# Scan order, opening by chunks, and the place of beside work in the attention rounds of a two-layer hybrid kernel

## The chip, the cores and the metric

The kernel runs on one core of a Trainium2 chip. The metric is the device time of one execution in microseconds. Before the change it is 11721.87 us, the median of three runs (11714.78 to 11722.49).

## What is computed

Input is `x`, four images of 64 x 64 pixels with 128 channels, all in fp32. Cut to what matters (weights left out of the argument lists):

```
# layer 0, on the group-normalised image: three selective scans over 4096 tokens
xz  = in_proj(x)                                  # 2 x 256 channels
y   = mamba(xz) + flip(mamba_b(flip(xz))) + unslice(mamba_s(slice(xz)))
x   = x + out_proj(y * silu(z))
#   mamba: conv of 4 taps, silu, delta = softplus(...), and the scan
#   h = h * exp(delta * A) + delta * u * B ;  y = sum_n h * C + D * u     (16 states)

# layer 1, on tokens t (4 images x 4096 tokens; the attention is over all 4096 of an image)
q   = ring(cos(layernorm(t) + theta))             # 16 heads of 8; q is query, key and value
a   = softmax(q q^T / sqrt(8)) q                  # per head, 4096 x 4096
x1  = layernorm(u + a w_comb + b)                 # u = layernorm(t)
t   = t + layernorm(x1 + w2 relu(w1 cos(x1[:8]) + b1) + b2)
# experts: each of 64 experts takes the 8 likeliest tokens of an image,
#   pools them, runs an MLP of 128-512-128, and adds the answer back to those tokens
```

## The kernel before

The work is a Python program that records instructions in an order of its own: generators yield small steps, and a `Pace` runs so many steps of each generator beside the attention rounds. What stands earlier in the program stands earlier in each engine's queue. The stages, with their place in the profiled execution:

1. **Head**, 0 to 2176 us. `Inputs` makes u, delta, B and C for all images (`pieces`, line 264; `of_chunk`, line 357) beside the scans of image 0 (`Scans.of_image`, line 457). Then `opening(0)` makes the tokens of image 0.
2. **Loops 0 to 2**, one per image (`Attention.loop`, line 875): attention of image b, beside it the scans of image b + 1, then `after(b - 1)` (line 985: output projection, feed-forward, the experts' logits), then `opening(b + 1)` (line 815).
3. **Loop 3**: attention of image 3 by query block; beside it `after(2)`, the experts' search and pooling for images 0 to 2, and `after(3)` for blocks that are done.
4. **Tail**, 250 us: the last block's `after`, the experts' answers, the scatter.

**A loop** has 1024 rounds, one for each group of 4 heads, block of 512 queries and block of 128 keys. In a round, `scores` (line 914) issues 4 score matmuls (line 924) into two PSUM tiles `s` and two exponentials `e` (line 929) of 128 x 1024 on ScalarE (ACT). `values` (line 932) issues 4 value matmuls (line 938, each executed as two) that add into one PSUM bank `acc`. Every 32 rounds `sums` copies `acc` to `av` (line 947), and three rounds later `store` writes it out by GpSimd's (POOL) queue (lines 953, 956). Lines 968 to 980 set the order of a round i: scores of round i + 1, values of round i, `av` at a block's end, stores, then `beside(i)`, which runs steps of the other generators. PSUM has three `s` tiles, one `acc` and one bank for all beside work (`Bank`, line 126): a step takes the bank with `yield PE`, so the caller knows that the step which follows is a piece of TensorE (PE) work, and `leave`s it after the copy out of it.

**The scans** go by order (0 forward, 1 backward, 2 slices), chunk of 1024 tokens (`T`; 4 chunks, `NC`), 8 blocks of 32 channels and 4 steps: 384 steps an image. A step loads delta and du two steps ahead on SyncE's (SP) queue (line 489), takes an exponential on ACT (line 503, `dA` or `delta`), and on VectorE (DVE) multiplies by B (line 510), scans (line 519) and multiplies by C (line 524). In two of four steps `total` (line 551) sums over states on PE into `y`: 16 matmuls, executed in one go with the step's exponential. `out` (line 556) adds D * u and stores a block of 32 channels by POOL's queue into one DRAM tile for each image and order. `product` (line 528) makes du for the next chunk beside the steps; its loads (line 540) follow on SP behind its last store. `early` (line 210) names the chunks whose du `Inputs` makes itself.

**The opening** of an image has 8 groups of 512 tokens. `tokens` (line 742) loads the three scans' sums and the gate `sz` (lines 750, 758, on SP), adds and multiplies them on DVE (line 763), projects by `out` on PE (line 771), normalises and starts the angles. `heads` and `rings` (lines 831, 841) make q: a transposition `qT` on PE (line 863), a split in two on DVE (lines 866, 867) and six stores on SP (line 871). In `beside` of `tile_kernel` (line 1478) the opening is run only once all scan steps of its image are done (`left == 0.0`); what is left after round 1023 is run between the loops (lines 1495 to 1499).

**`after`**, block by block: `co` (line 1041), `zt` (1062), `h` (1076, matmuls with 8 rows), `fo` (1087), `xT` (1109), `lg` (1119). The experts' pooling has `wt` (1254) and `pool` (1265). Each is one piece on PE between two yields. In loop 3 all this goes at 0.92 steps a round (line 1519), and what is left then runs behind the loop (`last.rest()`).

Of the kernel before, what the change touches and what calls it, by code (L numbers as in the profile page):

```python
# [23 lines left out]
SLICES = 16  # L24
T = 1024
# [183 lines left out]

def early(b, order, c):  # L210

    return b == 0 or (b == 1 and order == 0 and c < 2)
# [15 lines left out]
class Inputs:  # L228
# [35 lines left out]
    def pieces(self, images):  # L264

        for b in images:
            self.sz[b] = self.dram.tile([DI, L], F32, name=f"d_sz_{b}")
            yield self.norm(b)
            for order in range(3):
                if order == 2:  # L270
                    yield self.slices(b)
                for c in range(NC):
                    yield self.of_chunk(b, order, c)
                    third, at = divmod(order * NC + c, 3)
                    if at == 2:
                        yield self.gate(b, third)
# [156 lines left out]
class Scans:  # L433
# [6 lines left out]
    def __init__(self, tc, ctx, ws, ident, bank, dram):  # L440
        nc = self.nc = tc.nc
        self.ws, self.bank, self.dram = ws, bank, dram
        const = ctx.enter_context(tc.tile_pool(name="s_const", side="right", bufs=1))
        self.rows = ctx.enter_context(tc.tile_pool(name="s_rows", side="right", bufs=2))
        self.deep = ctx.enter_context(tc.tile_pool(name="s_deep", side="right", bufs=3))
        self.small = ctx.enter_context(tc.tile_pool(name="s_small", side="right", bufs=2))

        self.sel = const.tile([P, 2, 32], F32, name="sel")
        nc.vector.memset(self.sel, 0.0)
        for i in range(2):  # L450
            nc.vector.tensor_reduce(
                self.sel[:, i, 16 * i : 16 * i + 16], ident.rearrange("p (d n) -> p d n", n=NS2),
                mybir.AxisListType.X, ALU.add,
            )
        self.sums, self.steps, self.did = {}, {}, set()

    def of_image(self, b, made, alone=False):

        nc = self.nc
        self.steps[b] = 0  # L460
        for order in range(3):
            self.sums[b, order] = self.dram.tile([DI, L], F32, name=f"d_y_{b}_{order}")
        steps = [(order, c, k, j) for order in range(3) for c in range(NC) for k in range(8) for j in range(4)]
# [64 lines left out]
        def product(s):  # L528

            order, c, k, j = steps[s]  # L530
            part, turn = divmod(4 * k + j - 8, 3)
            chunk = (b, order, c + 1) if c + 1 < NC else (b, order + 1, 0) if order < 2 else (b + 1, 0, 0)
            if part < 0 or turn == 1 or chunk not in made or early(*chunk):
                return
            of, m, at = made[chunk], part // 4, part % 4 * (T // 4)
            cut = slice(m * P, (m + 1) * P), slice(at, at + T // 4)
            if turn == 0:
                for name in ("delta", "u"):
                    t = self.extra.tile([P, T // 4], F32, tag=f"x_{name}", name=f"x_{name}_{b}_{s}")
                    nc.sync.dma_start(out=t, in_=of[name][cut])  # L540
                    tiles["x", name] = t
            else:
                t, u = tiles.pop(("x", "delta")), tiles.pop(("x", "u"))
                nc.vector.tensor_mul(t, t, u)  # L544
                nc.gpsimd.dma_start(out=of["du"][cut], in_=t)  # L545
# [10 lines left out]
        def out(s, y):  # L556
# [10 lines left out]
            nc.vector.scalar_tensor_tensor(into, u, self.ws[order]["D"][:, k : k + 1], y, ALU.mult, ALU.add)  # L567
            to = self.sums[b, order][32 * k : 32 * k + 32]
            if order == 0:
                nc.gpsimd.dma_start(out=to[:, c * T : (c + 1) * T].rearrange("p (g t) -> g p t", g=4), in_=o)  # L570
                return
# [79 lines left out]
class Attention:  # L651
# [3 lines left out]
    def __init__(self, tc, ctx, w, gate, cols, ident, bank, dram, t1, w_out, sums, sz, x):  # L655
# [3 lines left out]
        self.w_out, self.sums, self.sz, self.x = w_out, sums, sz, x  # L659
# [51 lines left out]
        self.lag = 0  # L711
# [30 lines left out]
    def tokens(self, b, g, angles):  # L742
# [5 lines left out]
        cut, tiles = slice(g * 512, (g + 1) * 512), slice(g * 4, g * 4 + 4)  # L748
        x_g = self.piece([P, 4, C], "x_g", name=f"xr_{b}_{g}")
        nc.sync.dma_start(out=x_g, in_=xin[:, tiles, :])  # L750
        ys = []
        for m in range(2):
            rows = slice(m * P, (m + 1) * P)
            parts = []
            for i, src in enumerate([self.sums[b, order] for order in range(3)] + [self.sz[b]]):
                tag, bufs = ("y0", 2 * self.n) if i == 0 else (f"p{i - 1}", self.ahead)
                t = self.one.tile([P, 512], F32, tag=tag, bufs=bufs, name=f"y{i}_{b}_{g}_{m}")
                nc.sync.dma_start(out=t, in_=src[rows, cut])
                parts.append(t)
            yield  # L760
            y = parts[0]
            for t, op in zip(parts[1:], (ALU.add, ALU.add, ALU.mult)):
                nc.vector.tensor_tensor(y, y, t, op)
            ys.append(y)
# [26 lines left out]
        yield  # L791

# [82 lines left out]
    def loop(self, b, beside, by_block=False):  # L875


        nc = self.nc
        self.context[b] = self.dram.tile([P, L], F32, name=f"d_ctx_{b}")
# [64 lines left out]
        def sums(j, qb, i):  # L944

            av = self.mid.tile([P, QB], F32, tag="av", name=f"av_{b}_{j}_{qb}")
            nc.scalar.copy(av, accs.pop((j, qb)))  # L947
# [20 lines left out]
        for i, (j, qb, kc) in enumerate(rounds):  # L968
# [4 lines left out]
            values(i)  # L973
            if kc == NT - 1:
                sums(j, qb, i)
# [4 lines left out]
            beside(i)  # L980
        for i in sorted(later):
            later[i]()
        self.whole[b] = L // QB

    def after(self, b, gs=range(L // QB), to=None):
# [68 lines left out]
        def second(g):  # L1054
# [6 lines left out]
            for k in range(4):  # L1061
                nc.tensor.transpose(ps[:D, k * P : (k + 1) * P], z[:, g * 4 + k, :], self.ident)
# [11 lines left out]
            for f in range(4):  # L1074
                ps = yield from self.bank.take(f"h_{b}_{g}_{f}")
                nc.tensor.matmul(ps, self.w1[:, f * P : (f + 1) * P], zT, start=True, stop=True)  # L1076
# [7 lines left out]
            for k in range(4):  # L1084
                ps = yield from self.bank.take(f"fo_{b}_{g}_{k}")
                for f in range(4):
                    nc.tensor.matmul(  # L1087
                        ps[:, :C], h[:, f, k * P : (k + 1) * P], self.w2[:, f, :], start=(f == 0), stop=(f == 3)
                    )
# [18 lines left out]
            for k in range(4):  # L1108
                nc.tensor.transpose(ps[:, k * P : (k + 1) * P], u[:, k, :], self.ident)
# [9 lines left out]
            nc.tensor.matmul(ps[rows], self.gate, xT, start=True, stop=True)  # L1119
# [286 lines left out]
class Pace:  # L1406
# [4 lines left out]

    def run(self, share):
        self.credit += share
        while self.credit >= 1 and not self.done:
            self.credit -= 1
            self.then = next(self.parts, self)
            self.done = self.then is self
# [6 lines left out]
def tile_kernel(tc, ctx, x, in_proj_w, dirs, out_proj_w, attn, gate, weight1, weight2, out):  # L1424
# [32 lines left out]
    block = Attention(tc, ctx, attn, gate, cols, ident, bank, dram, t1, w_out, scans.sums, inputs.sz, x)  # L1457
# [14 lines left out]
    with tc.manual_schedule():  # L1472
        last = Pace()
        n = 3 * NC * NB
        for b in range(nb - 1):
            opens = Pace(block.opening(b + 1))

            def beside(i):
# [4 lines left out]
                following.run(min(1.3, max(0.5, left / max(1, 860 - i))))  # L1483
                other = last if not last.done else opens if left == 0.0 else None
                if other is None:
# [23 lines left out]
    with tc.manual_schedule():  # L1509
# [9 lines left out]
        block.loop(nb - 1, lambda i: last.run(0.92), True)  # L1519
        last.rest()  # L1520
    loop.close()
# [49 lines left out]
```

## Time and profile before

The profiled execution took 11713.44 us; its span is 11711.7 us. The other runs are the median and range above.

| stage | from - to (us) | PE busy | DVE busy | ACT busy | granted clock |
|---|---|---|---|---|---|
| head | 0 - 2175.6 | 1421.3 | 2016.3 | 1150.2 | 0.80 |
| loop 0 | 2175.6 - 4570.2 | 2224.1 | 2058.1 | 2326.4 | 0.98 |
| between | 4570.2 - 4614.7 | 8.2 | 37.1 | 7.3 | 0.63 |
| loop 1 | 4614.7 - 6976.9 | 2237.4 | 2065.1 | 2297.6 | 0.98 |
| between | 6976.9 - 7021.3 | 8.2 | 37.1 | 7.3 | 0.62 |
| loop 2 | 7021.3 - 9345.4 | 2217.1 | 1890.2 | 2258.2 | 0.98 |
| loop 3 | 9348.0 - 11461.8 | 2073.0 | 360.7 | 1939.3 | 0.99 |
| tail | 11461.8 - 11711.7 | 127.6 | 86.1 | 32.3 | 0.67 |

Over the whole span PE is busy 88%, ACT 86%, DVE 73%. A busy time is the union of an engine's instructions; both matmuls and exponentials overlap their successors, so a duration is longer than the time from one start to the next, and a share near 100% does not say that an engine never waits. The idle columns of the groups and the starts in the timeline say that. "<-" names what ended a wait. PEld is the loading of weights ahead of a matmul.

### The profile page before, as it was taken

What the parts mean: (1) busy time and instruction counts of PE and PEld (TensorE: products, weight loads), DVE (VectorE), ACT (ScalarE), POOL (GpSimd) and SP (SyncE); (2) the same over time, 40 slices, a digit from 0 to 9 for tenths busy, and PEclk for the clock granted to TensorE, in tenths of its full rate; (3) what the DMA queues carried; (4) which work ended last, traced back from release to release, by engine and by line L of the source; (5) the groups of instructions that cost most, each with busy time, mean ns of one, the idle gap of its engine ahead of it and who ended that gap; (6) DMA issues with size and microseconds to landing.
All of it is one profiled execution on the core that took longest, in us unless ns stands there. A gap on an engine that the chain in (4) does not pass through costs nothing.

```text
span 11711.7 us, 181745 instructions
## 1 busy us (share of the span) xinstructions
PE 10319.3 (88%) x68038; PEld 3430.9 (29%) x68038; DVE 8550.7 (73%) x8743; ACT 10019.7 (86%) x10604; POOL 3373.1 (29%) x4017
## 2 busy tenths in 40 slices
PE   6677674699999997999999979999999999999995
PEld 2222231222222232333333222333332223333323
DVE  7999998898988877998898879989887321101113
ACT  4565563699999997999999989999999999999992
POOL 5525362231323222324244223243341111000011
PEclk8888786799999998999999989999999999999997
DMA  6777777655565556665656566565555322222125
GB/s 186 219 222 209 212 209 204 174 152 154 150 155 147 145 161 173 158 157 147 156 140 154 150 176 168 152 153 142 150 138 137 120 93 67 75 70 76 59 73 187
DMA packets 835819, 1747.47 MB, mean 149 GB/s; under 512 B 141070, under 2 KB 373574, under 8 KB 834678
## 3 DMA queue, kind: packets, MB, share of 16 engines
q1 hardware_dynamic: 649438, 1318.65, 42.3%
q0 software_dynamic: 144000, 307.48, 8.5%
q10 hardware_dynamic: 41496, 109.71, 3.5%
q8 instruction: 534, 8.75, 0.3%
q14 instruction: 351, 2.88, 0.1%
HBM read 1379.76 MB, written 355.47 MB: 148 GB/s over the span
## 4 chain that ended last, share of the span: by engine, by line
PE 58%; DVE 13%; ACT 10%; issue 9%; DMA 8%; SPq 1%; POOL 0%; ACTq 0%; DVEq 0%; POOLq 0%
PE acc L938 33%; PE s L924 15%; ACT e L929 7%; DVE h L519 7%; PE y L551 4%; DMA delta<-d_delta 3%; DVE dB L510 2%; DMA du<-d_du 1%; PE fo L1087 1%; DVE du L510 1%; PE h L1076 1%; DMA y<-d_y 1%; PE cv L387 1%; DMA w<-in_L_ffn_weight_dram 1%; ACT dA L503 1%
## 5 line engine op out<-in xcount | busy, mean ns | idle before, releaser
L929 ACT ACTIVATE e<-s 128x1024 f32<-128x1024 f32 x8192 | 7777.3, 1102 | 357.9 <-PE s L924 313.0
L938 PE MATMUL acc<-e,val 128*32 128x512 f32 x32768 | 5676.3, 612 | 79.5 <-ACT av L947 78.7
L924 PE MATMUL s<-qm,key 32*128 32x512 f32 x16384 | 2784.7, 501 | 370.5 <-ACT e L929 310.5
L521 POOL COPY ends<-h 128x1 f32<-128x1 f32 x1152 | 1608.5, 1396 | 2597.6 <-DVE h L519 2590.9
L924 PEld LDWEIGHTS s<-qm,key 32*128 32x128 f32 x16384 | 1067.4, 183 | 3619.9 <-issue 1948.1
L938 PEld LDWEIGHTS acc<-e,val 128*32 128x32 f32 x32768 | 1028.4, 108 | 2009.7 <-issue 1015.4
L519 DVE TENSOR_TENSOR_SCAN h<-delta,ends,du 128x1024 f32<-128x1024 f32 x576 | 1353.5, 2350 | 86.3 <-ACT delta L503 77.1
L519 DVE TENSOR_TENSOR_SCAN h<-dA,ends,dB 128x1024 f32<-128x1024 f32 x576 | 1353.3, 2350 | 21.4 <-ACT dA L503 17.8
L503 ACT ACTIVATE dA<-delta,A 128x1024 f32<-128x1024 f32 x768 | 938.6, 1222 | 482.0 <-DMA delta<-d_delta 426.4
L510 DVE TENSOR_TENSOR dB<-du,B 128x1024 f32<-128x1024 f32 x768 | 931.8, 1213 | 549.8 <-PE y L551 370.1
L503 ACT ACTIVATE delta<-delta,A 128x1024 f32<-128x1024 f32 x768 | 938.9, 1222 | 75.3 <-PE y L551 68.4
L510 DVE TENSOR_TENSOR du<-du,B 128x1024 f32<-128x1024 f32 x768 | 925.6, 1205 | 28.7 <-DMA B<-d_bc 28.7
L524 DVE TENSOR_TENSOR dB<-h,C 128x1024 f32<-128x1024 f32 x768 | 939.6, 1223 | 0.0
L524 DVE TENSOR_TENSOR du<-h,C 128x1024 f32<-128x1024 f32 x768 | 939.4, 1223 | 0.1
L551 PE MATMUL y<-du,sel 128*32 128x256 f32 x6144 | 738.5, 404 | 184.1 <-DVE du L524 183.9
L551 PE MATMUL y<-dB,sel 128*32 128x256 f32 x6144 | 733.5, 400 | 91.6 <-DVE dB L524 40.9
L953 POOL DMA_DIRECT2D d_ctx<-av x512 | 260.7, 521 | 922.5 <-ACT av L947 912.7
L387 PE MATMUL cv<-xn,conv 128*128 128x512 f32 x1024 | 488.4, 632 | 20.0 <-DVE xn L322 20.0
L580 POOL DMA_DIRECT2D d_y<-o x512 | 329.6, 673 | 550.8 <-DVE o L567 489.9
L545 POOL DMA_DIRECT2D d_du<-x_delta x272 | 155.2, 571 | 1105.4 <-DVE x_delta L544 1029.2
L519 DVE TENSOR_TENSOR_SCAN h<-delta,du 128x1024 f32<-128x1024 f32 x192 | 439.2, 2287 | 13.1 <-ACT delta L503 7.1
L519 DVE TENSOR_TENSOR_SCAN h<-dA,dB 128x1024 f32<-128x1024 f32 x192 | 439.2, 2287 | 11.9 <-ACT dA L503 10.6
(245 smaller groups left out, 6450.8 us busy)
## 6 DMA issues: line engine op xcount, KB each, us to landing
delta<-d_delta SPq DMA_DIRECT2D x768, 512.0 KB
du<-d_du SPq DMA_DIRECT2D x576, 512.0 KB
du<-d_du ACTq DMA_DIRECT2D x192, 512.0 KB
key<-d_q SPq DMA_DIRECT2D x352, 256.0 KB
d_u<-u POOLq DMA_DIRECT2D x48, 1024.0 KB, 7.1
d_delta<-r POOLq DMA_DIRECT2D x48, 1024.0 KB, 6.5
B<-d_bc SPq DMA_DIRECT2D x96, 512.0 KB
C<-d_bc SPq DMA_DIRECT2D x96, 512.0 KB
```

The costliest lines, as they stand in the source:

```text
L387: nc.tensor.matmul(ps[:, cut], w["conv"][:, k, m * P : (m + 1) * P], reads(k, g), start=(k == 0), stop=(k == 3))
L503: nc.scalar.activation(tiles["delta", s], t, AF.Exp, scale=A)
L510: nc.vector.tensor_mul(tiles["du", s], du, spread[order, c, "B", j % 2])
L519: nc.vector.tensor_tensor_scan(h, dA, dB, first, ALU.mult, ALU.add)
L521: nc.gpsimd.tensor_copy(ends[order, c][:, at : at + 1], h[:, T - 1 :])
L524: nc.vector.tensor_mul(dB, h, spread[order, c, "C", j % 2])
L551: nc.tensor.matmul(y[32 * g : 32 * g + 32, : T // 4], self.sel[:, j // 2, :], hC[:, 256 * g : 256 * g + 256], start=(j == 0), stop=(j == 3),)
L580: nc.gpsimd.dma_start(out=to.rearrange("p (i j) -> p i j", i=SLICES)[:, :, at : at + n], in_=rows.rearrange("p (i j) -> p i j", i=SLICES),)
L924: nc.tensor.matmul(s_ps[:, k, :], keys[f"{i // 4}"][rows, cut].bitcast(F32R), queries[j, qb][rows, :].bitcast(F32R), start=True, stop=True,)
L929: nc.scalar.activation(e, s_ps, AF.Exp, scale=1.0 / math.sqrt(D))
L938: nc.tensor.matmul(accs[j, qb][32 * k : 32 * k + 32, :], v[:, k * VW : k * VW + 32], es[i][k // 2][:, k % 2, :], start=(kc == 0), stop=(kc ...
L953: nc.gpsimd.dma_start(out=self.context[b][h * D : h * D + D, cut], in_=av[32 * k : 32 * k + D, :])
```

## The change

Four things are changed together.

- **Order of scans.** Images 1 to 3 scan backward, slices, forward (`ORDERS`); `Inputs` makes their chunks in that order. The forward order's sums go to one DRAM tile a chunk instead of one for the image.
- **Opening by chunks.** `tokens` no longer waits for the whole scan: it goes on when the blocks stored (`stored`) reach chunk c of the forward order, two blocks later for all but the last chunk. It waits some rounds more between loads and sums (`settle(2)`). `beside` runs the opening as soon as `after` is done, in the same slots as `after`, and the scans are spread to round 890 instead of 860.
- **Place of beside work.** In all four loops `beside(i)` stands between the scores of round i + 1 and the values of round i. The store of `av` is moved with it.
- **Loop 3.** PE pieces of `after` are cut in two by `pause` (a `yield PE` while `cut` is set): `zt`, `h`, `fo`, `xT`, `lg`; `h` and `lg` become two matmuls of 256 columns. `turn` runs up to three steps a round with at most one PE piece, and no PE piece in every third round until 831. `av` is copied by DVE.

```diff
+ORDERS = {0: (0, 1, 2), 1: (1, 2, 0)}
...
+def orders(b):
+    return ORDERS[min(b, 1)]
...
-    return b == 0 or (b == 1 and order == 0 and c < 2)
+    return b == 0 or (b == 1 and order == orders(b)[0] and c < 2)
...
-        for order in range(3):
+        for order in range(1, 3):
             self.sums[b, order] = self.dram.tile([DI, L], F32, name=f"d_y_{b}_{order}")
+        for c in range(NC):
+            self.sums[b, 0, c] = self.dram.tile([DI, T], F32, name=f"d_y_{b}_0_{c}")
...
+            self.stored[b] += 1
+            if order == 0:
+                to = self.sums[b, order, c][32 * k : 32 * k + 32]
+                nc.gpsimd.dma_start(out=to.rearrange("p (g t) -> g p t", g=4), in_=o)
+                return
...
+        c, part = divmod(g, T // 512)
+        while self.scans.stored[b] < min(8 * (2 * NC + c + 1) + 2, 8 * 3 * NC):
+            yield WAIT
...
             yield
+            yield from self.settle(2)
             y = parts[0]
...
+    def pause(self):
+        if self.cut:
+            yield PE
...
-            nc.scalar.copy(av, accs.pop((j, qb)))
+            (nc.vector.tensor_copy if by_block else nc.scalar.copy)(av, accs.pop((j, qb)))
...
                 scores(i + 1)
-            values(i)
-            if kc == NT - 1:
-                sums(j, qb, i)
...
             if i in later:
                 later.pop(i)()
             beside(i)
+            values(i)
+            if kc == NT - 1:
+                sums(j, qb, i)
...
             for k in range(4):
+                if k == 2:
+                    yield from self.pause()
                 nc.tensor.transpose(ps[:D, k * P : (k + 1) * P], z[:, g * 4 + k, :], self.ident)
...
-                nc.tensor.matmul(ps, self.w1[:, f * P : (f + 1) * P], zT, start=True, stop=True)
+                for part in range(2):
+                    cols = slice(part * QB // 2, (part + 1) * QB // 2)
+                    if part:
+                        yield from self.pause()
+                    nc.tensor.matmul(ps[:, cols], self.w1[:, f * P : (f + 1) * P], zT[:, cols], start=True, stop=True)
...
                 for f in range(4):
+                    if f == 2:
+                        yield from self.pause()
                     nc.tensor.matmul(
                         ps[:, :C], h[:, f, k * P : (k + 1) * P], self.w2[:, f, :], start=(f == 0), stop=(f == 3)
...
+    def turn(self, share, free):
+        self.credit = min(self.credit + share, 3.0)
+        while self.credit >= 1 and not self.done and (free or self.then is not PE):
+            free = free and self.then is not PE
+            self.step()
...
-                following.run(min(1.3, max(0.5, left / max(1, 860 - i))))
-                other = last if not last.done else opens if left == 0.0 else None
-                if other is None:
+                following.run(min(1.3, max(0.5, left / max(1, 890 - i))))
+                other = opens if last.done else last
+                if other.done:
                     return
...
-        block.loop(nb - 1, lambda i: last.run(0.92), True)
+        block.loop(nb - 1, lambda i: last.turn(1.5, i % 3 > 0 or i > 830), True)
         last.rest()
+        block.cut = False
```

## The prediction

> **What bounds the kernel now.** I read, in this order, the page's chain and groups, the busy times by stage, the idle time of ScalarE by group in each stage, and two short timelines. Stages are cut where the first and last exponential `e` (line 929) of each attention loop start. The busy times of loop 0, the gap behind it, loop 1 and loop 3 (PE, PEld, DVE, ACT, POOL, clock, DMA):
> ```profile
> 2175.60:4570.20 2394.60, 2224.08 (x15724) 693.08 (x15722) 2058.07 (x1727) 2326.37 (x2494) 678.36 (x897) 0.98 0.59 153
> 4570.20:4614.70 44.50, 8.17 (x54) 3.53 (x54) 37.05 (x51) 7.25 (x8) 15.28 (x15) 0.63 0.73 220
> 4614.70:6976.90 2362.20, 2237.41 (x15932) 718.54 (x15930) 2065.14 (x2093) 2297.57 (x2467) 769.79 (x938) 0.98 0.59 154
> 9348.00:11461.80 2113.80, 2072.97 (x13528) 651.40 (x13526) 360.74 (x936) 1939.30 (x2109) 174.77 (x307) 0.99 0.24 73
> ```
> ACT has the least room in the loops. Its durations overlap, so I count spacings of neighbours that follow without a wait: 0.904 us for an `e`, 1.040 for a scan exponential (line 503), 0.465 for the `av` copy, 1.295 for a table load. Loop 3: 2113.8 - 2047 x 0.904 (1850.5) - 31 x 0.465 (14.4) - table loads and the choice's exponentials (21.2) = **228 us idle**. Loop 0: 2394.6 - 1850.5 - 410 x 1.040 (426.4) - 14.4 - 9.2 = **94**; loop 1 likewise **91**, loop 2 **94**. The gap after loop 0 holds 6.6 us of ACT work, so **38** idle, that after loop 1 the same, that after loop 2 one. Together 584 us that a change of order could win; the head (2175.6) and most of the tail (249.9) are outside it.
>
> ACT's groups, two lines of loop 0 and one of loop 3 (busy time, mean ns, then the idle time ahead of the group and what ended it; gaps under 0.15 us are not in it):
> ```profile
> L929 ACT ACTIVATE e<-s 128x1024 f32<-128x1024 f32 x2047 | 1968.8, 1137 | 65.8 <-PE s L924 65.5
> L503 ACT ACTIVATE dA<-delta,A 128x1024 f32<-128x1024 f32 x205 | 258.9, 1263 | 28.3 <-DMA delta<-d_delta 28.2
> L929 ACT ACTIVATE e<-s 128x1024 f32<-128x1024 f32 x2047 | 1909.3, 1057 | 174.3 <-PE s L924 135.0 <-PE h L1076 39.2
> ```
> So ACT waits for scores from PE, and in loops 0 to 2 also for a delta load (28, 24, 20 us). Why PE is late is seen in loop 3, PE alone; from 9705.33 an `h` matmul stands in the round:
> ```profile
> 9701.66 0.50 PE L924 MATMUL s<-qm,key 32*128 32x512 f32 x4
> 9702.09 1.47 PE L938 MATMUL acc<-e,val 128*32 128x512 f32 x8
> 9703.49 0.50 PE L924 MATMUL s<-qm,key 32*128 32x512 f32 x4
> 9703.92 1.47 PE L938 MATMUL acc<-e,val 128*32 128x512 f32 x8
> 9705.33 0.69 PE L1076 MATMUL h<-zT,w 8*128 8x512 f32 x1
> ...
> 9706.61 1.06 PE L938 MATMUL acc<-e,val 128*32 128x512 f32 x8
> 9707.61 0.75 PE L924 MATMUL s<-qm,key 32*128 32x512 f32 x4
> ```
> The weight loads and ACT beside it:
> ```profile
> 9702.09 0.14 PEld L938 LDWEIGHTS acc<-e,val 128*32 128x32 f32 x4 [0.24 <-issue]
> 9702.51 0.14 PEld L938 LDWEIGHTS acc<-e,val 128*32 128x32 f32 x4 [0.28 <-ACT e L929]
> ```
> ```profile
> 9706.79 3.77 ACT L929 ACTIVATE e<-s 128x1024 f32<-128x1024 f32 x4 [0.66 <-PE h L1076]
> ```
> A plain round lasts 1.83: scores 0.43, values 1.40. The values wait 0.4 us in their middle for the second `e`. Where both are ready (9706.61 to 9707.61) values take 1.00. So PE has **0.40 us** of slack a round, but ahead of the values' second half; after the values there is none, since the next `e` starts as soon as its scores end. A piece put after the values costs ACT its whole length. By spacing in loop 3: `fo` 1.088 us, `h` 0.85 (0.53 and 0.32 that the next scores take longer), `co` 0.641, `zt` 0.530, `xT` 0.585, `lg` 1.003, `wt` 1.032, `pool` 1.035. Times the counts 60, 60, 30, 15, 14, 14, 24, 24 that is 215, of the 228 idle.
>
> **The change, part by part.** Counts are from the order of both built programs.
>
> *Swap and halves in loop 3.* Ahead of the values a piece is free up to 0.40. `fo`, 120 halves of 0.544: 17. `wt` and `pool` stay whole, 48 x 0.634: 30. `co` 30 x 0.241: 7. `lg` 30 halves of 0.50: 3. Halves of `zt` and `xT` (0.27, 0.29): 0. A half `h` is unknown: 0.425 if all of it halves, 0.585 if the 0.32 stays; 120 of them cost 3 to 22, I take 12, the middle. Sum 69, and 11 for the small gaps that are there now: **80 instead of 228, gain 148**. Pacing lets at most one piece into a round and none into every third until 831, and all pieces are out by round 960, so nothing piles up.
> A rule that speaks against halving: the Trainium skill, "TensorE: Matmul & The Clock Gate", section on LDWEIGHTS, makes a weight load cost its columns over 1.2 whatever streams behind it. By it a second load for 128 columns would add some 0.11 us (an estimate), and a half `h` would cost 0.53 rather than 0.425. The `h` load is 0.18 us in this trace, mostly under another matmul.
>
> *`av` copy to DVE in loop 3.* ACT loses 32 x 0.465 = **15 us**. On DVE a 512-wide copy out of PSUM is 0.69 (line 1112), no longer than `av` on ACT (0.67). DVE is busy 361 of 2114 us, so it starts soon after the values end, ahead of the next values' second half. A queued 4 us search would delay it; two or three of those a loop are nothing. POOL's stores still follow three rounds later.
>
> *Swap in loops 0 to 2.* The scan's sums `y` last 1.37 and mostly share a round with one exponential (1.040): 206 + 190 + 172 of them at 0.33 make 188, against 178 waited for scores. With 0.40 more they fit. Left are `out` and `qT` pieces, 5, 7 and 9 us by the count: **gain 178 - 21 = 157**. The delta waits (72) stand at the starts of chunks, where B, C, delta and du load together; they and the 29 us of small gaps (94 + 91 + 94 - 178 - 72) stay. The later `av` copy behind an exponential, 31 a loop, is covered by the two `e` before it.
>
> *Opening by chunks.* In the new program nothing of the opening is left between the loops (now 8 `qT` transposes and 5 exponentials each): **gain 76**. The openings' loads, DVE chains and stores move from rounds 832-1023 and the gap to 640-1000, beside a scan at nearly full pace. Two prices. DVE: its instructions times their spacings make 148.5, 153.5 and 146.2 us in rounds 768-831 against 144.6, 144.8 and 142.7 for ACT, 17 too many; now it is 151.2 against 139.8 in 960-1023 of loops 0 and 1. SP: `y` loads wait for a free tile and the q stores (line 871) for DVE, and the scan's delta loads queue behind. In 4250-4620 such stores held SP 88 us in 7 waits (longest 29.2), with no delta stall until the gap. But there the scan went at half pace. Today a delta load is issued 17 us ahead of its use (median; least 5.5), although SP already stops 72 times in 1850 us for the du store (line 540). So 0 to 88 a loop; I take 20, near the end that the 72 harmless stops speak for: **cost 60**. The added settling rounds take DVE's wait for `y` loads away (18 us at 4300-4570), which ACT did not see.
>
> *Order of scans, head, tail.* Same instructions, other order; the head's DVE is 93% busy with image 0, which keeps its order: 0. In the tail the search of block 6 and one `xT` and `lg` go into the loop, so the `d_ctx` stores, which stand behind POOL's norm until 11468.8, start some 3 us earlier and DVE's search (3.9) no longer stands in the chain; but weight loads start earlier beside the small hops: 0 to 12, I take **5**.
>
> Sum: 148 + 15 + 157 + 76 - 60 + 5 = 341, and ACT's idle time in the loops falls from 584 to 263. The profiled execution took 11713.4 us (span 11711.7, launch around it 1.7), 8 below the median of 11721.9: 11713 - 341 = **11372 us**, 3.0% under the median.
>
> **Rivals.**
> 1. *DVE becomes the bound beside the scans.* It is busy 2058 of 2394 us; as rounds shorten to ACT's sum, its sums per 64 rounds (126 to 140) stand against 142 to 146 for ACT, some 90%, and it waits in order for `y`, PSUM and POOL. For: 2.25 to 2.4 us a round now, with little slack. Against: DVE is released earlier by `y`, which now runs ahead of the values. Then the 157 is lost: 11372 + 157 = 11529.
> 2. *The swap hides nothing*, as PE's wait only moves. For: PE busy 98% in loop 3. Against: the 1.00 and 1.40 above. Halves would not help, as the sum of pieces stays. Left 76 + 15 + 5 - 60 = 36: 11677.
> 3. *Slower: SP's queue.* An opening has 16 groups of `y` loads and 16 groups of q stores that can hold SP. The gains without the 60 are 401, over 96 holds: from **4.2 us a hold** on, paid in full by ACT, the kernel is slower; at 6 us it is 576 - 401 = 175 slower, 11888. For: the 29 us wait. Against: the 17 us lead.
> That the change doesn't do what it says is out: the new order shows pieces ahead of the values and empty gaps.
>
> **How the numbers follow.** Forecast 0.72, rival 1 0.14, rival 2 0.06, rival 3 0.04, and 0.04 for more than the bounds below. Low end: opening free (-60), `h` halves 3 (-9), small gaps gone (-40), tail 12 (-7): 11372 - 116 = 11256. High end: rival 1, 11530; an opening at 88 a loop (+204) lies outside with it, at 11576. Faster by over 0.2% 0.95, within 0.2% 0.01 (about what a measurement of this kernel can tell from no change), slower 0.04.
>
> **What would show it.** Right: no stretch between loops with ACT under half busy; loop 3 near 1952 us, loops 0 to 2 near 2360, 2337 and 2297; ACT's wait for scores at 60 to 80 in loop 3 and under 20 in each other. Wrong step: waits of `dA` for delta growing past 50 a loop in rounds 640-1000 (SP), or scores waiting although no piece stands ahead of them (rival 2), or DVE over 95% there (rival 1). `h` halves next to whole idle gaps of 0.2 would show the fixed part.

## The result, and the profile after

The changed kernel takes **11535.9 us** (median of four runs, 11533.28 to 11538.26) against 11721.28 for the kernel before, measured beside it (11714.78 to 11722.49): ratio **0.9843, 95% interval 0.9826 to 0.986**. The forecast was 11372, with a range up to 11530: the direction was right, about half of the gain came.

Loop 0, the gap behind it, loop 1 and loop 3 after (the same view and columns as the first one of the prediction):
```profile
2180.26:4555.15 2374.89, 2125.14 (x15682) 630.12 (x15682) 2042.08 (x1740) 2320.51 (x2489) 679.12 (x907) 0.98 0.60 156
4555.15:4557.91 2.76, 2.50 (x14) 0.58 (x14) 2.76 (x2) 1.61 (x3) 0.00 (x0) 1.00 0.91 220
4557.91:6919.20 2361.29, 2135.75 (x16054) 670.92 (x16056) 2101.78 (x2144) 2302.34 (x2472) 771.61 (x953) 0.98 0.61 157
9251.18:11285.40 2034.22, 1963.45 (x13684) 631.72 (x13682) 393.49 (x995) 1924.42 (x2079) 177.35 (x314) 0.98 0.25 76
```
The gap is gone (44.5 to 2.76). Loop 0 lost 20 us, loop 1 one, loop 3 80, and with 2374.9, 2361.3 and 2034.2 all three are above the 2360, 2337 and 1952 of the forecast. ACT's groups, two of loop 0 and one of loop 3 after:
```profile
L951 ACT ACTIVATE e<-s 128x1024 f32<-128x1024 f32 x2047 | 1964.6, 1128 | 49.8 <-PE s L946 49.2 <-ACT dA L511 0.2
L511 ACT ACTIVATE dA<-delta,A 128x1024 f32<-128x1024 f32 x203 | 253.5, 1249 | 31.0 <-DMA delta<-d_delta 31.0
L951 ACT ACTIVATE e<-s 128x1024 f32<-128x1024 f32 x2048 | 1905.3, 1061 | 109.6 <-PE s L946 99.5 <-ACT e L951 0.3
```
In loop 0 the waits of `e` read 65.8 us before and 49.8 after, but in both some 26 of it stand ahead of the loop's first exponential, in the head (26.2 and 26.5). Inside the loop the wait for scores fell from 39 to 23 us (under 20 was forecast), inside loops 1 and 2 from 38 and 37 to 38 and 31, in loop 3 the waits of `e` from 174.3 to 109.6 (60 to 80). By the count of spacings (0.904 an `e`, 1.040 a scan exponential, 0.465 an `av` copy, 1.295 a table load) ACT's idle time went as follows:

| us of idle ACT | before | forecast | after |
|---|---|---|---|
| loops 0 to 2, rounds 0 to 639 | 119 | | 107 |
| loops 0 to 2, rounds 640 to 1023 | 162 | | 143 |
| loops 0 to 2, both | 281 | 182 | 250 |
| the gaps behind them | 77 | 1 | 6 |
| loop 3 | 228 | 80 | 162 |

With 14 us of `av` copies gone from ACT in loop 3, and the head 5 and the tail 1 longer, this makes 175 on the spans (11711.7 to 11536.5).

What fills the 162 in loop 3 is not the pieces' length alone. Eighteen idle stretches of over 1.2 us hold 70.0 of it; before there were two, with 2.6. What PE waited for in loop 3 after (total, times, longest):
```profile
PE s L946 <- ACT e L951: 16.6, 10, 2.7
PE xT L1141 <- DVE x1r L832: 15.1, 4, 4.2
PE acc L960 <- DVE av L969: 12.4, 14, 3.2
PE wt L1290 <- DVE chosen L1278: 8.9, 2, 4.6
PE co L1063 <- DVE cT L1055: 7.9, 2, 6.9
PE h L1104 <- DVE h L1107: 4.8, 2, 3.2
```
All but the first line are waits for DVE at the head of PE's queue: for an operand that DVE has not made yet (`xT`, `wt`, `co`), or for a PSUM bank that DVE has not emptied yet (`acc` behind `av`, `h` behind `h`). One of them in the timeline after:
```profile
10157.41 4.42 DVE L1278 SCALAR_TENSOR_TENSOR chosen<-chosen,prob 128x4096 f32<-128x4096 f32 x1
...
10161.89 1.96 PE L1290 MATMUL wt<-diagonal,chosen 64*128 64x64 f32 x8 [4.63 <-DVE chosen L1278]
10163.79 1.93 PE L960 MATMUL acc<-e,val 128*32 128x512 f32 x8
10165.65 0.80 PE L946 MATMUL s<-qm,key 32*128 32x512 f32 x4
10166.55 1.94 ACT L951 ACTIVATE e<-s 128x1024 f32<-128x1024 f32 x2 [7.17 <-PE s L946]
```
DVE makes the choice for 4.42 us, `wt` waits 4.63 for it, values and scores stand behind `wt` although their operands are ready, and ACT stands 7.17 us.

### The profile page after: what moved, and what is told of

Same layout as the page of the kernel before. It is cut to its first block, busy times and chain, and to the rows that moved or that the text cites. A ratio compares the mean times of both kernels' runs of the same rounds, so it can differ in the third digit from the quotient of the medians.

```text
span 11536.5 us, 182284 instructions
## 1 busy us (share of the span) xinstructions
PE 9889.9 (86%) x68358; PEld 3255.8 (28%) x68358; DVE 8566.2 (74%) x8775; ACT 9999.8 (87%) x10572; POOL 3273.9 (28%) x4017
## 4 chain that ended last, share of the span: by engine, by line
PE 35%; ACT 23%; DVE 17%; issue 16%; DMA 8%; POOL 1%; SPq 1%; ACTq 0%; DVEq 0%; POOLq 0%
PE acc L960 20%; ACT e L951 20%; PE s L946 10%; DVE h L527 8%; DMA delta<-d_delta 3%; DVE dB L518 2%; DMA du<-d_du 2%; PE cv L393 1%; DVE du L518 1%; ACT dA L511 1%; ACT delta L511 1%; PE fo L1117 1%; DVE du L532 1%; PE h L1104 1%; PE y L560 1%
## 5 line engine op out<-in xcount | busy, mean ns | idle before, releaser
L960 PE MATMUL acc<-e,val 128*32 128x512 f32 x32768 | 5251.6, 616 | 107.3 <-ACT av L969 93.8
L946 PE MATMUL s<-qm,key 32*128 32x512 f32 x16384 | 2650.4, 500 | 587.6 <-ACT e L951 557.8
L946 PEld LDWEIGHTS s<-qm,key 32*128 32x128 f32 x16384 | 1012.7, 184 | 4448.9 <-issue 2490.5
L529 POOL COPY ends<-h 128x1 f32<-128x1 f32 x1152 | 1492.0, 1296 | 2649.8 <-DVE h L527 2646.1
L960 PEld LDWEIGHTS acc<-e,val 128*32 128x32 f32 x32768 | 971.2, 109 | 1607.2 <-issue 788.6
L560 PE MATMUL y<-du,sel 128*32 128x256 f32 x6144 | 506.4, 403 | 169.5 <-DVE du L532 169.0
L560 PE MATMUL y<-dB,sel 128*32 128x256 f32 x6144 | 515.1, 408 | 70.3 <-DVE dB L532 39.7
L393 PE MATMUL cv<-xn,conv 128*128 128x512 f32 x1024 | 491.2, 635 | 26.2 <-DVE xn L328 26.2
```

The costliest lines, as they stand in the source:

```text
L393: nc.tensor.matmul(ps[:, cut], w["conv"][:, k, m * P : (m + 1) * P], reads(k, g), start=(k == 0), stop=(k == 3))
L529: nc.gpsimd.tensor_copy(ends[order, c][:, at : at + 1], h[:, T - 1 :])
L560: nc.tensor.matmul(y[32 * g : 32 * g + 32, : T // 4], self.sel[:, j // 2, :], hC[:, 256 * g : 256 * g + 256], start=(j == 0), stop=(j == 3),)
L946: nc.tensor.matmul(s_ps[:, k, :], keys[f"{i // 4}"][rows, cut].bitcast(F32R), queries[j, qb][rows, :].bitcast(F32R), start=True, stop=True,)
L960: nc.tensor.matmul(accs[j, qb][32 * k : 32 * k + 32, :], v[:, k * VW : k * VW + 32], es[i][k // 2][:, k % 2, :], start=(kc == 0), stop=(kc ...
```

## The experiments

Theory at the start: the swap pays in loop 3 but not in the scan loops, and in loop 3 the dense pace (1.5 steps in two rounds of three, no settling) makes PE wait for DVE. Rivals: DVE is the bound beside the scans; SP's queue is held by the opening; halves cost more than their part of the whole. "Loop 3" is the time from its first to its last exponential. The kernel before, run beside the experiments, took 11717.69 (first four), 11712.72 (the next four) and 11713.01 us (`f1` to `f3`); those up to `f3` are one run each, the last three are timed.

### Swap in loops 0 to 2 alone

```diff
+            swapped = not by_block
+            if not swapped:
                 values(i)
...
             beside(i)
+            if swapped:
+                values(i)
```


> Before, with the swap in loops 0 to 2 alone. The prediction's theory (the scan's sums y cost 1.37 us a round ahead of the next scores) expects ACT's wait for scores in these loops to fall from 178 to some 21 us, time near 11556. Rival (y runs in other columns of the array while the values wait for the second e, so it costs about 0.9 and is already covered by the round's exponential): loops 0 to 2 change by less than 25 us in all, near 11690 to 11715; only the 40 out and 24 qT pieces gain, at most 0.4 us each.

Measured: **11713.07**, 4.6 less than the kernel before beside it, where 157 less was forecast from this term; the rival's range holds. The loops' idle time is 282 us against 281 (loop 0 is 9 shorter, loop 1 13 longer, loop 2 3 shorter). Two scan rounds in the timeline show why. Before:
```profile
2341.97 0.49 PE L924 MATMUL s<-qm,key 32*128 32x512 f32 x2 [0.47 <-ACT e L929]
2342.39 1.11 PE L938 MATMUL acc<-e,val 128*32 128x512 f32 x6
2343.28 0.39 PE L551 MATMUL y<-dB,sel 128*32 128x256 f32 x2
2343.34 0.60 PE L938 MATMUL acc<-e,val 128*32 128x512 f32 x2
...
2344.73 0.50 PE L924 MATMUL s<-qm,key 32*128 32x512 f32 x4
2345.16 1.07 PE L938 MATMUL acc<-e,val 128*32 128x512 f32 x8
2346.16 1.01 PE L924 MATMUL s<-qm,key 32*128 32x512 f32 x4
2347.09 1.11 PE L938 MATMUL acc<-e,val 128*32 128x512 f32 x6
```
With the swap:
```profile
2340.95 0.51 PE L924 MATMUL s<-qm,key 32*128 32x512 f32 x2 [0.47 <-ACT e L929]
2341.38 0.64 PE L551 MATMUL y<-dB,sel 128*32 128x256 f32 x8
...
2342.27 1.04 PE L938 MATMUL acc<-e,val 128*32 128x512 f32 x8
2343.24 0.50 PE L924 MATMUL s<-qm,key 32*128 32x512 f32 x4
...
2345.64 0.50 PE L924 MATMUL s<-qm,key 32*128 32x512 f32 x2 [0.47 <-ACT e L929]
```
Two rounds with one `y` and one scan exponential take 4.70 us before (2342.39 to 2347.09) and 4.69 with the swap (2340.95 to 2345.64). ACT needs 4 x 0.904 + 1.040 = 4.66 for them, so it sets the pace in both. Before, `y` starts 0.89 after the values began, beside the last two of their eight matmuls (2343.34), where scores start 1.40 after them: `y` already lies in part beside the values' second half. Over the 568 rounds with a `y` the medians are 1.39 from `y` to the next scores and 2.27 from the values to these scores. So `y` adds some 0.87 to a round, not the 1.37 of the forecast, and that is less than the scan's exponential (1.040). With the swap `y` takes 0.89 and the values behind it 0.98, so that it adds 0.47. The 0.40 of the forecast is thus saved on PE, but ACT did not wait for it. The swap only moves PE's wait: its waits of scores for ACT grow from 132.7 to 205.0 us in loop 0.

### Opening by chunks and the order of scans alone

The first two parts of the change as they stand in its diff, without the swap and with the old loop 3; the lines that let the opening go beside the scans:
```diff
+        while self.scans.stored[b] < min(8 * (2 * NC + c + 1) + 2, 8 * 3 * NC):
+            yield WAIT
...
-                other = last if not last.done else opens if left == 0.0 else None
+                other = opens if last.done else last
```

> Before, with the new order of scans and the opening by chunks alone; work beside rounds and loop 3 as before. Theory: the two gaps go (76 us of ACT idle time), rounds 640 to 1023 then show 40 to 60 us of ACT idle time a loop from late delta loads and late PE pieces; together 11620 to 11650. If the opening beside scans cost only the 20 us a loop that were predicted, near 11600.

Measured: **11633.42**, 84 less, inside the first bounds. The gaps' 77 idle us fall to 7; rounds 640 to 1023 have 157 idle against 162, so the opening beside a scan at full pace costs nothing on balance. What it costs is seen in the delta waits (`dA` waits 63 in these rounds against 30); all other idle time there falls by as much, from 132 to 94.

### Swap in loop 3 alone, pieces whole

```diff
-            values(i)
+            swapped = by_block
+            if not swapped:
+                values(i)
...
+            if swapped:
+                values(i)
```


> Before, with the swap in loop 3 alone; pieces whole, 0.92 steps a round, av on ACT. Theory (0.40 us of each piece is hidden ahead of the values): ACT idle 228 falls by 60 x 0.40 (fo) + 60 x 0.40 (h) + 104 x 0.40 (the others), about 90, loop 3 near 2023 us, time near 11622. If the swap hides nothing, loop 3 stays at 2114.

Measured: **11611.47**, 106 less; loop 3 is 2009.9, 13 better than expected, its idle time 124.5, with one stretch over 1.2 us. The 0.40 of slack ahead of the values is real: whole `fo` pieces cost 37.8 in all (60 x 0.63), and whole `h` 22.9, where they cost some 63 and 50 before.

### After, with whole pieces at the dense pace

`turn(1.5)`, the swap and `av` on DVE stay.
```diff
-        self.cut = by_block
...
-                for part in range(2):
-                    cols = slice(part * QB // 2, (part + 1) * QB // 2)
-                    if part:
-                        yield from self.pause()
-                    nc.tensor.matmul(ps[:, cols], self.w1[:, f * P : (f + 1) * P], zT[:, cols], start=True, stop=True)
+                nc.tensor.matmul(ps, self.w1[:, f * P : (f + 1) * P], zT, start=True, stop=True)
```
(and `lg` likewise)

> After, with whole pieces in loop 3 (no pause, h and lg in one matmul); swap, pacing and av on DVE stay. The prediction's theory (halves cost half): pieces would cost 118 us instead of 69, so loop 3 is 50 us longer than in the changed kernel, 2084. Rival (a half keeps a fixed part of about 0.1 us, fo 0.642 instead of 0.544): 118 against some 80, 40 us longer; and if what is left over in loop 3 is PE waiting for DVE in a dense pace, whole pieces change that part little, so 2060 to 2080.

Measured: **11600.49**; loop 3 is 2084.7, 75 more than with the swap alone, though ACT has 14 less to do. Its idle time outside long stretches is 126 (121 with the swap alone); 19 stretches over 1.2 us hold 86.6. So it is the dense pace, together with `av` on DVE, that costs. Against the changed kernel it is 50 longer, the theory's figure; 34 of it lie outside long stretches (126 against 92), the other 17 in them.

### After, with an even pace for the halves

```diff
-        block.loop(nb - 1, lambda i: last.turn(1.5, i % 3 > 0 or i > 830), True)
+        block.loop(nb - 1, lambda i: last.turn(1.25, True), True)
```


> The changed kernel, with one line altered: in loop 3 the pieces run at an even 1.25 steps a round instead of 1.5 steps in two rounds of three (no round is kept empty). Theory (pace): the some 60 us in 13 stalls of 2.9 to 8.8 us in which TensorE waits for an input of DVE or a DMA come from the dense pace; spread evenly, most of them go, and loop 3 falls from 2034 to 1965-1990, the time to 11465-11495. Rival (halves): the stalls hang on the chain of pieces itself, and the halves' spacings (fo 0.642, h 0.52) are what costs; loop 3 stays at 2015-2045 and the time at 11515-11545. A second rival: without empty rounds pieces pile up against the 0.40 of slack; loop 3 over 2050.

Measured: **11503.42**; loop 3 is 1998.4 and both are 8 over the theory's bounds: the long stretches fall from 70.0 to 36.3 us, seven are left, among them one of 11.1 at round 994.

### After, with whole pieces at the old pace, av on ACT

```diff
-        block.loop(nb - 1, lambda i: last.turn(1.5, i % 3 > 0 or i > 830), True)
+        block.loop(nb - 1, lambda i: last.run(0.92), True)
```
(with whole pieces, and `nc.scalar.copy` for `av`)

> The changed kernel with the last loop's pieces whole (h and lg by one matmul, fo, zt, xT in one go), at the 0.92 steps a round of the kernel before, and the av copy on ScalarE; the values stay behind the pieces in all loops, and the openings by chunks. So it leaves out the halving, the new pace and the av copy on DVE. Theory (pace): halves, pace and av copy together brought nothing; loop 3 is the 2010 of the run that had the swap in the last loop alone, loops 0 to 2 are as in the changed kernel, and the time is 11536 - 2034 + 2010 = 11512 (by the sum of the single runs 11531 at most). Rival (halves pay): it is slower than the changed kernel by 20 us or more.

Measured: **11508.71**, 27 less than the changed kernel; loop 3 is 2008.3, without one long stretch. So three parts of the change to loop 3 (halves, pace, `av` on DVE) together made it slower than the swap alone does.

### After, with rounds ahead of the next y loads

```diff
-        yield
+            yield
+            yield from self.settle(2 - m)
```


> The changed kernel, with rounds let pass between the sums of y on DVE and the next y loads on SP in the openings, so that these loads are issued once their tiles are free. Theory (SP holds): the 47 us that ScalarE waits for delta in rounds 640 to 1023 of loops 0 to 2 come from loads that hold SP while they wait for a tile; they fall to 25 or less and the time by 20 to 30, to 11506-11516. Rival: the waits stand at the starts of chunks and come from the loads' own time; they stay at 40 or more and the time within 8 of 11536. Other side: the opening gets longer, and what does not fit comes between the loops, 10 or more slower.

Measured: **11517.41**, inside the bounds, but not clean: the additional step also acts in the head, which gets 15.6 longer, while loop 0 gets 17.5 shorter. These are not 15 us of scans, as an expectation below has it: the head holds one scan exponential more (399 against 398). It is repeated below without that step.

### After, with av on ACT

```diff
-            (nc.vector.tensor_copy if by_block else nc.scalar.copy)(av, accs.pop((j, qb)))
+            nc.scalar.copy(av, accs.pop((j, qb)))
```


> The changed kernel with the av copy of the last loop on ScalarE again instead of DVE. Theory of the prediction: ScalarE takes 32 copies at 0.465, 15 us, and the time rises to 11551. Rival: the values wait in PSUM for DVE's late copies (acc behind av on DVE: 33 us of waits on TensorE and its weight loads in loop 3), which goes; the time falls by 5 to 20.

Measured: **11549.01**, by the total near the first theory; but loop 3 got 7.6 **shorter** (2026.6), and loops 0 to 2, whose instructions are the same in both, together 19 longer. Loop 3 repeats within 1.5 us where its instructions are the same (2034.2, 2034.2 and 2033.0 in the changed kernel and the two runs that only add rounds to the openings); loops 0 to 2 differ by more. So the 7.6 count, and the total says nothing on `av`. A pair below tries it without the dense pace.

### One more settling round in loop 3, even pace

```diff
+        block.lag = 1
-        block.loop(nb - 1, lambda i: last.turn(1.5, i % 3 > 0 or i > 830), True)
+        block.loop(nb - 1, lambda i: last.turn(1.5, True), True)
+        block.lag = 0
...
         nc.vector.scalar_tensor_tensor(w, w, 0.0, prob[rows], ALU.is_lt, ALU.mult)
         yield
+        yield from self.block.settle(4)
```


> The changed kernel, last loop only: one more round let pass between each result of DVE and the TensorE piece that reads it (the settling rounds that loops 0 to 2 have, and four behind the choice), at 1.5 steps in every round, so that all pieces still end by round 954. Theory (halves are worth 36 once PE does not stand waiting: fo 37.8 to 24.4, h 23.5 to 5, lg 8 to 5): loop 3 comes down from 2008 with whole pieces by 36 and by the 14 of the av copy, to some 1958, the prediction's 1952; the time is 11455 to 11475. Rival (halves and waits are one thing: the pieces' chains are too long to be kept apart, so the stalls move): loop 3 stays over 1990, the time over 11495.

Measured: **11481.65**, 7 over its bounds but far under the rival's; loop 3 is 1969.5, 12 over the figure expected, and the long stretches hold 12.9 us. The pieces stand as dense as in the changed kernel (in 409 rounds, the last 954, against 407 and 952).

### The same with av on ACT

The line of `av` as in the last run but one, on top of the run above.

> The same as the run with one more round, with the av copy on ScalarE again. Theory of the prediction: plus 15 against that run. Rival: the values' wait for av on DVE behind a search (one of 10.3 us in the run with even halves, 22 us in all) goes, and the two cancel: within 6 of it. If av on DVE costs more than it saves, this run is the faster one.

Measured: **11466.02**; loop 3 is 1966.6, shorter by 2.9 though ACT has 32 copies more (14 us). On DVE the copy leaves ACT idle for 98.2 in loop 3, on ACT for 80.4: what ACT saves it waits for, since the next block's values need the one `acc` bank, and DVE copies it when its queue gets there (waits of up to 3.4 us on PE, against 0.9). Of the total's 16, thirteen come from elsewhere: loop 1, the same in both, differs by 10.

### After, with rounds ahead of the q stores too

```diff
+        yield from self.settle()
         for x, t in enumerate((high, low, high, low, low, high)):
```


> The changed kernel with rounds let pass ahead of the next y loads, as in the settled run (11517), and also between DVE's split of the angles and the q stores that SP issues. Theory (SP holds): the waits of dA for delta left in rounds 640 to 1023 (about 33 us in that run) come from q stores that hold SP for DVE; they fall by 10 to 20, the time to 11497-11510. Rival: what is left are chunk starts and the scan's own stores: within 6 of 11517.

Measured: **11534.04**, 17 more than the settled run, outside both bounds. `dA` waits in rounds 640 to 1023 are 33 in it and 35 in the settled run, against 47 in the changed kernel; the difference lies in loops 1 and 2 (7 and 18 us), in waits without one place, and such differences stand between runs of the same instructions too. Nothing follows for the q stores.

### Timed: the best, the best with settled loads, the best without the swap in loops 0 to 2

> The fastest kernel so far once more, now timed: the changed kernel with one more settling round and an even 1.5 steps in the last loop, and the av copy on ScalarE. Theory: loop 3 holds its 1967 (80 us idle, the figure of the prediction for swap and halves), and the time is 11460 to 11472, a ratio of 0.978 to 0.979 to the kernel before.

> The same with rounds let pass between the sums of y on DVE and the next y loads on SP, now without an additional step in the head (the settled run of before had moved 15 us of scan from loop 0 into the head). Theory (SP holds cost something): 10 to 25 us under the kernel timed beside it. Rival: the 19 us of the single look were head and scatter of the loops (single looks of the same loops 0 to 2 differ by up to 10 us each): within 8 us of it.

```diff
             ys.append(y)
+            yield from self.settle(2 - m)
```


> The same as the first of these three with the values ahead of the other work again in loops 0 to 2; in the last loop they stay behind it. So it takes the swap out of the three loops in which the prediction set it at 157 us, with the opening now beside the scan. Prediction: 157 us slower, about 11620. Rival (the scan's y already lie under the values' wait for the second exponential): within 10 us of it. Between: with the openings beside the scan the out and qT pieces and the copies gain from it, 10 to 40 us.

```diff
+            if not by_block:
+                values(i)
...
             beside(i)
+            if by_block:
                 values(i)
```

| kernel (four runs each; before 11721.66) | median | range | ratio, 95% interval |
|---|---|---|---|
| even pace, a settling round, av on ACT | 11476.13 | 11472.86 to 11478.81 | 0.979 [0.9775, 0.9804] |
| and rounds ahead of the next y loads | **11463.98** | 11459.32 to 11472.80 | 0.978 [0.9764, 0.9796] |
| the first, swap in loop 3 only | 11480.19 | 11474.63 to 11486.54 | 0.9793 [0.9779, 0.9808] |

The first is the same kernel as the run of 11466.02, and 4 over its bounds. Its loop 3 and what PE waits for there:
```profile
9259.74:11226.27 1966.53, 1931.38 (x13684) 623.07 (x13682) 373.16 (x964) 1934.27 (x2109) 177.21 (x314) 1.00 0.26 78
```
```profile
PE s L946 <- ACT e L951: 17.1, 11, 2.7
PE acc L960 <- ACT av L969: 16.1, 28, 0.9
PE xT L1141 <- DVE x1r L832: 1.4, 3, 0.6
PE wt L1291 <- DVE chosen L1278: 0.6, 1, 0.6
```
The waits for DVE (49 us in five lines after the change) are down to 2; the values' wait for the bank is now one for ACT's copy, 16.1 us in short pieces. ACT is idle for 80.9 us, one stretch over 1.2. The swap in loops 0 to 2 is worth 4 us with overlapping ranges, also with the openings beside the scans: no difference that these runs can tell. The settled loads are worth 12 by the medians, inside the theory's bounds. The ranges just meet; what speaks for it is the place. `dA` waits for delta in rounds 640 to 1023 fall from 51 to 30 us, in loops 0 and 1, not in loop 2. Idle time in rounds 0 to 639 rises by 12 in the same pair, so that some 10 of the 21 are left over the loops. Such a hold in the changed kernel, first on SP's queue, then on ACT:
```profile
6430.91 11.12 SPq L773 DMA_DIRECT2D y<-d_y  x3
6442.44 0.32 SPq L773 DMA_DIRECT2D y<-d_sz  x1
6442.85 0.54 SPq L497 DMA_DIRECT2D delta<-d_delta  x1
```
```profile
6443.91 1.14 ACT L951 ACTIVATE e<-s 128x1024 f32<-128x1024 f32 x1
6449.76 1.15 ACT L511 ACTIVATE dA<-delta,A 128x1024 f32<-128x1024 f32 x1 [4.71 <-DMA delta<-d_delta]
```
Three `y` loads hold SP for 11.12 us, the delta load is issued right behind them, and ACT waits 4.71 for it.

## Why the prediction was wrong, point by point

- **Swap and halves in loop 3, gain 148, 80 idle: the sum came out without PE's waits for DVE, the sentence under it did not hold.** In the kernel with the settling round the loop has 80.9 idle us, which is 228 less 147. By piece: `fo` 22 (forecast 17), `wt` and `pool` 26 (30), `co` 6 (7), `lg` 3 (3), `zt` and `xT` 5 (0), small gaps 16 (11); `h` 1 instead of 12, with some 6 more among the small gaps (120 x 0.05). The terms are off by up to 11 and cancel: that the sum is so near is in part luck. A whole `h` ahead of the values (swap in loop 3 alone), and a half (the kernel with the settling round):
```profile
9553.70 0.51 PE L924 MATMUL s<-qm,key 32*128 32x512 f32 x4
9554.04 1.02 PE L1082 MATMUL h<-zT,w 8*128 8x512 f32 x2
9554.99 1.07 PE L938 MATMUL acc<-e,val 128*32 128x512 f32 x8
9555.99 0.51 PE L924 MATMUL s<-qm,key 32*128 32x512 f32 x4
```
```profile
9589.83 0.50 PE L946 MATMUL s<-qm,key 32*128 32x512 f32 x4
9590.17 0.59 PE L1104 MATMUL h<-zT,w 8*128 8x256 f32 x2
9590.69 1.07 PE L960 MATMUL acc<-e,val 128*32 128x512 f32 x8
9591.69 0.50 PE L946 MATMUL s<-qm,key 32*128 32x512 f32 x4
```
  The half takes 0.52 from start to start, but the scores ahead of it only 0.34 instead of 0.43. Its round lasts 1.86, against 1.43 for scores and values alone (0.43 + 1.00): it adds 0.43, half of the 0.85 that the whole one adds (2.28). ACT needs 1.81 for the round (2 x 0.904), so a half costs it some 0.05.

  The rule that the prediction weighed here (the Trainium skill, "TensorE: Matmul & The Clock Gate", section on LDWEIGHTS: a weight load takes its columns over 1.2, in ns) had given the estimate of 0.53 for a half `h`. These runs do not bear that estimate out: on the footing of the 0.85 that was halved, the half adds 0.43. The `h` load itself shows 0.18 us in the trace, where the rule has 0.11 for its 128 columns.

  The step that failed is "**Pacing lets at most one piece into a round and none into every third until 831, and all pieces are out by round 960, so nothing piles up**". It counted PE's pieces a round and not the time between a piece and its operand. At 1.5 steps and no settling rounds, a matmul is issued about one round behind the DVE work that feeds it. In the changed kernel idle ACT was 162, 70 of it in long stretches. With one settling round (and four behind the choice) the stretches hold 13, though the pieces stand as dense as before; at an even 1.25 steps without it they hold 36. So the distance from DVE's work to the piece is shown as the cause, and the number of pieces a round is not. The run with the settling round also fills the third round that had been kept empty; the settling round with that pattern kept was not run.
- **`av` to DVE, gain 15: nothing.** ACT's 14 us went, and came back as waits: loop 3 is 2.9 shorter (and at the dense pace 7.6) with the copy on ACT. The step "it starts soon after the values end" overlooked that DVE's queue holds norms and a search in front of the copy; "two or three of those a loop are nothing" was mis-sized: in the changed kernel the values wait for the copy 14 times, 12.4 us on PE, and at the even pace once for 10.3 us behind a search.
- **Swap in loops 0 to 2, gain 157: nothing** (4 in the timed pair, 5 in the single run). The step that failed is "**The scan's sums `y` last 1.37 and mostly share a round with one exponential (1.040): 206 + 190 + 172 of them at 0.33 make 188**". 1.37 is a stretch of time, not what a `y` adds; the values ahead of it give back 0.5 of it. The 178 that it was to explain was misread, too. 62.9 of it are the waits of each loop's first `e` in the kernel before, and these stand in the head and in the two gaps, whose idle time is the term of 76:
```profile
2175.61 3.77 ACT L929 ACTIVATE e<-s 128x1024 f32<-128x1024 f32 x4 [26.24 <-PE s L924]
4614.71 1.94 ACT L929 ACTIVATE e<-s 128x1024 f32<-128x1024 f32 x2 [18.18 <-PE s L924]
7021.30 1.94 ACT L929 ACTIVATE e<-s 128x1024 f32<-128x1024 f32 x2 [18.48 <-PE s L924]
```
  Inside the loops ACT waited 115 for scores, and the small gaps that the prediction put at 29 are 92. By the piece that PE ran last before the wait, some 63 us stand behind an `out` of the opening and only some 25 behind a `y`. That 188 was near 178 was chance. In these loops rival 2 (PE's wait only moves) was right, in loop 3 it was wrong.
- **Gaps, gain 76: 71.** Right.
- **Opening beside the scans, cost 60: about nothing on balance** (157 idle against 162 with the opening alone, 143 in the changed kernel). The holds on SP exist, and the settled loads win 12 back by the medians; but the kernel before paid as much in these rounds for other waits. Rival 3 was wrong: it priced a hold in full, and the waits of `dA` sum to 47 us over three loops, under the 50 a loop that was to show it.
- **Tail, gain 5: 1 lost. Head, 0: 5 lost** (2175.6 to 2180.3). What these come from was not looked into.
- **Rival 1 (DVE the bound beside the scans), 11529** is close to the result, by another way: the 157 were not lost to DVE beside the openings; with the swap alone, where the openings stood as before, they did not come either. Its sign did not come: DVE is busy 85, 88 and 75% in rounds 640 to 1000 of loops 0 to 2, not over 95%. What fills the 107 idle us of rounds 0 to 639 stays open.

## What to carry to other kernels

Price a piece by what it adds from start to start with its neighbours on both sides, not by its own duration: if the work ahead of it gets shorter by its coming, it already has a hiding place, and a new one wins nothing. An engine that issues in order needs, besides a free slot, an operand that is ready when the slot comes: before a piece is moved closer to its producer or its pace is raised, count the rounds between them, and give the distance back as empty steps (here, with the pieces as dense as before, the stalls fell from 70 to 13 us). Before a copy that frees the only buffer of the critical loop is moved off the engine that is the bound, ask when the other engine's queue will get to it: here the move won nothing. And before waits are summed over a stage, see whether the first of them lies ahead of it.

## What the runs showed of the hardware that was not expected

- Matmuls of `y` behind the values start 0.89 us after these began, beside the last two of the values' eight matmuls; the same 16 take 0.89 from start to the next group with the swap, and 1.39 to the scores without it (medians of 568 rounds).
- Half an `h` (256 columns, 8 rows) takes 0.52 from start to start and a whole one 0.95, but the scores ahead of each are 0.09 shorter, so that two halves add 2 x 0.43 and the whole one 0.85: halving it cost PE nothing. Half an `fo` takes 0.64 where half of 1.088 was taken, 0.1 more, and halving paid all the same: `fo` cost ACT 22 us instead of 37.8.
- Loops 0 to 2, with the same instructions in the same order, differ by up to 11.5 us a loop between runs of different kernels, and the same kernel took 11466.0 in one set of runs and 11476.1 (median) in another. Differences under some 15 us between single runs say little without their place in the trace; loop 3 repeated within 1.5.
